# Attention probabilities fetched in three half-key buffers over two loop steps, and the value products ahead of a 512-column query product

## The chip, the cores and the metric

The kernel runs on one core of a Trainium2 chip. The metric is the device time of one execution in microseconds (us); lower is better. TensorE (PE) multiplies matrices, VectorE (DVE), ScalarE (ACT) and GpSimd (POOL) work on elements, and SyncE (SP) issues nearly all DMA transfers of the part that is changed. Each engine takes its instructions in the order of the program.

## The reference

Two layers over x of shape 16 x 256 x 256 (16 sequences of 256 tokens), all in float32. Each is x + s * silu(f), with s and f computed from the layer norm of x. In layer 0, s is a complex linear recurrence and f a two-matrix network with gelu. In layer 1, f is a linear layer with gated low-rank experts, and s is the attention that the change touches:

```
q = x @ Wq                                  # 16 heads of 128 + 64 (rotary)
c_kv, k_rope = x @ Wkv_a                    # 64 latent + 64 rotary columns, shared by the heads
kv = rmsnorm(c_kv) @ Wkv_b                  # keys and values of each head
scores = q . k / sqrt(192), causal mask
attn = softmax(scores)
out = (attn . v) @ Wo
```

The kernel folds Wkv_b into Wq and Wo, so that all heads share one 128-wide key (64 latent, 64 rotary) and one 64-wide value, the latent itself.

## The kernel before

Layer 0 takes the first 270 us or so. Layer 1 is one software pipeline, unrolled by the loop `for i in range(LAST)` (line 1643). A **chunk** is two sequences (512 tokens); there are 8. A **group** is four heads of a chunk; there are 4 per chunk, 32 in all. A **unit** is one group for one of the two sequences, b = 0 or 1. Step i of the loop handles unit i, so even steps have b = 0 and odd steps b = 1, and r = i mod 8 is the place in the chunk. Group m is units 2m and 2m+1.

What a step writes, in program order, as far as it matters here:

1. On odd steps `fetch` of group (i-3)/2, four DMAs on SP.
2. `score_pack(u, 0)`: the **first scores**, two products of 256 and 224 columns into a PSUM bank `sc`; DVE masks them and takes the row maxima, ACT takes exponentials into `pr`.
3. `turn(w, 1)`, `turn(w, 2)`: DVE transposes, by 32 x 32 blocks, two thirds of the normalised probabilities of the unit before, w, into `turned`.
4. `query_mm(n, 3)` on even steps: a **query product** of 512 columns, `pq<-xnT,wlat`; `query_lat` (ACT) moves it to `qg`. (On odd steps it is `query_mm(n, 0)`.)
5. `score_pack(u, 1)`: the **second scores**, 192 + 160 + 128 columns.
6. `turn(w, 0)`, the last third, which follows the second scores in DVE's order, and `send(w)`: four SP DMAs, `far<-turned`, to a DRAM buffer.
7. On even steps `query_move(n)`: eight SP DMAs, `qg<-qrot`, that bring the rotary rows of the queries to their partitions, and then `values_of` of group (i-4)/2.
8. `score_pack(u, 2)`: the **third scores**, 96 + 64 + 32 columns, and then what the place r asks for (`pm`, `pg`, `tp`, `pkv`, `po`).

`far` lays the transposed probabilities out so that a second set of DMAs, `pT<-far`, brings them back with keys on partitions: rows 0 to 63 of `pT` belong to b = 0 and rows 64 to 127 to b = 1. The index y = 0 or 1 tells which 64 keys of each block of 128. `pT` of a group is one tile with one buffer, filled by four DMAs of 384 KB in the order (y, b) = (0,0), (0,1), (1,0), (1,1). `values_of` multiplies it with the values `rowv` in 64 x 64 quarters of the array, for key blocks z = 0 to 3 of 64 keys; block z reads half y = z mod 2. Here z = 0, 1, 2, 3 have 512, 384, 256 and 128 columns:

```
for z, c0 in enumerate((0, 64, S, S + 64)):
    n0 = 64 * z
    heads = q.pT[:, z % 2, :, c0 : c0 + S - n0].rearrange("p (a hh) q -> p a hh q", hh=2)
```

So a group's b = 1 half is sent on step 2m+2, fetched at the start of step 2m+3, and used on step 2m+4. PE's order is fixed by the `InOrder` helper (line 53), and so is that of the other engines; the profile books everything recorded through it under line 53. PSUM has five banks `m1` taken in turn (`pq`, `av`, `po` and others) and three banks `sc`.

Of the kernel before, what the change touches and what calls it, by code (L numbers as in the profile page):

```python
# [11 lines left out]
F32 = mybir.dt.float32  # L12
# [6 lines left out]
P = 128  # L19
B, S, D = 16, 256, 256  # L20
# [21 lines left out]
def tile_two_layers(ctx: ExitStack, tc: tile.TileContext, d: dict, out: bass.AP):  # L42
# [175 lines left out]
    sp = InOrder(nc.sync)  # L218
# [5 lines left out]
    def m1(name, shape):  # L224
        return place["pool"].tile(shape, F32, tag=place["tag"], name=name)
# [84 lines left out]
    def key_chunk(ch):  # L310
        k = chunks[ch]
        pk = m1(f"pk_{ch}", [P, CH])
        for j in range(TPC):
            pe.transpose(pk[:, j * P : (j + 1) * P], k.row[:, j, :], ident)
        k.kT = ak.tile([P, CH], F32, tag="kT", name=f"kT_{ch}")
        ac.copy(k.kT, pk)
# [62 lines left out]
    G = 4  # L379
# [60 lines left out]
    with ExitStack() as l0:  # L440
# [106 lines left out]
        def tiny(name, n=1):  # L547
            return w0.tile([P, n], F32, tag=name, name=name)
# [44 lines left out]
        f = tiny("f")  # L593
# [12 lines left out]
        for k in range(1, 8):  # L606
            c, s = rot[:, k - 1, 0:1], rot[:, k - 1, 1:2]
# [10 lines left out]
        for k in range(8):  # L618
            n = 1 << k
            c, s = rot[:, k, 0:1], rot[:, k, 1:2]  # L620
# [124 lines left out]
        def recur_out(ch, g, w, ve, ge):  # L745

            swapped(w, g)
            h = a2.tile([P, S], F32, tag="hs", name=f"hs_{ch}")
            ve.tensor_tensor(h, g, ct, ALU.mult)
            ge.tensor_tensor(h, h, w, ALU.subtract)  # L750
            return h
# [512 lines left out]
        h = recur_out(ch, g, w, v0, g0)  # L1264
# [35 lines left out]
    pp = ctx.enter_context(tc.tile_pool(name="p1", bufs=2))  # L1300
# [29 lines left out]
    def gate_end(ch, jp):  # L1330
        k = chunks[ch]
        g = k.g2[:, 2 * jp : 2 * jp + 2, :]
        ve.scalar_tensor_tensor(g, g, 1.0, k.h, ALU.add, ALU.mult)
# [31 lines left out]
    def score_pack(u, pi):  # L1365
        k, b, pack = chunks[u.ch], u.b, PACK[pi]
        if pi == 0:
            u.nm = sm1.tile([P, NQ], F32, tag="nm", name=f"nm_{u.n}", bufs=3)
            u.sr = sm1.tile([P, NQ], F32, tag="sr", name=f"sr_{u.n}", bufs=3)
        qg = groups[u.i // 2].qg  # L1370
        sc = ps_sc.tile([P, CH], F32, tag="sc", name=f"sc_{u.n}_{pi}")
        for a, o in pack:
            pe.matmul(
                sc[:, o : o + 32 * (a + 1)], qg[:, b * NQ + a, :, :].rearrange("p h q -> p (h q)"),
                k.kT[:, b * S : b * S + 32 * (a + 1)], start=True, stop=True,
            )
        ends = [o + 32 * (a + 1) for a, o in pack]
        step = ends[1] - ends[0]
        n = len(pack)
        assert ends == [ends[0] + step * z for z in range(n)]  # L1380
        if ends[0] - 32 + step * n <= CH:
            diag = sc[:, ends[0] - 32 : ends[0] - 32 + step * n].rearrange("p (n s) -> p n s", n=n)[:, :, 0:32]
        else:
            diag = sc[:, ends[0] - step : ends[-1]].rearrange("p (n s) -> p n s", n=n)[:, :, step - 32 : step]
        ve.tensor_tensor(diag, diag, bc(kmask, n), ALU.add)
        for a, o in pack:
            ve.tensor_reduce(
                u.nm[:, a : a + 1], sc[:, o : o + 32 * (a + 1)], AX.X, ALU.max, negate=True
            )
        for a, o in pack:  # L1390
            w = 32 * (a + 1)
            ac.activation(
                u.pr[:, OFF[a] : OFF[a] + w], sc[:, o : o + w], AF.Exp,
                bias=u.nm[:, a : a + 1], accum_out=u.sr[:, a : a + 1],
            )

    def normalise(u, packs):
        blocks = [a for pi in packs for a, _ in PACK[pi]]
        lo, hi = min(blocks), max(blocks) + 1
        ve.reciprocal(u.sr[:, lo:hi], u.sr[:, lo:hi])  # L1400
        for a in blocks:
            v = u.pr[:, OFF[a] : OFF[a] + 32 * (a + 1)]
            gp.tensor_scalar(v, v, u.sr[:, a : a + 1], 1.0, ALU.mult, ALU.mult)
# [29 lines left out]
    def new_pT(u):  # L1433
        u.pT = pp.tile([P, G, 3, P], F32, tag="turned", name=f"pT_{u.n}", bufs=2)

    def fetch(n):

        q = groups[n]
        q.pT = pp.tile([P, 2, G, 3 * P], F32, tag="pT", name=f"pT_{n}", bufs=1)
        far = q.far.rearrange("b (y k) s h z q -> y b (k s) (h z q)", y=2)  # L1440
        for y in range(2):
            for b in range(2):
                sp.dma_start(
                    q.pT[64 * b : 64 * b + 64, y].rearrange("p h q -> p (h q)"), far[y, b]
                )

    def turn_here(u, z):

# [32 lines left out]
    def values_of(n):  # L1481

        q = groups[n]
        ch, g = divmod(n, NG)
        k = chunks[ch]
        av = [m1(f"av_{ch}_{g}_{b}", [P, 2, S]) for b in range(2)]
        for z, c0 in enumerate((0, 64, S, S + 64)):
            n0 = 64 * z
            heads = q.pT[:, z % 2, :, c0 : c0 + S - n0].rearrange("p (a hh) q -> p a hh q", hh=2)
            for b in range(2):  # L1490
                rows = slice(64 * b, 64 * b + 64)
                for hh in range(2):
                    pe.matmul(
                        av[b][64 * hh : 64 * hh + 64, :, n0:S], k.rowv[rows, z, :],
                        heads[rows, :, hh, :], start=(z == 0), stop=(z == 3),
                    )
        k.attT.append(a2.tile([P, 2, CH], F32, tag="attT", name=f"attT_{ch}_{g}", bufs=6))
        for b in range(2):
            ac.copy(k.attT[g][:, :, b * S : (b + 1) * S], av[b])
# [143 lines left out]
    for i in range(LAST):  # L1643
        ch, r = divmod(i, PER)
        odd = i % 2 == 1
        u, w = units[i], units[i - 1] if i else None
        here = w is not None and w.i >= LAST - 2
        n = (i + 3) // 2 if odd else (i + 2) // 2
        n = n if n < len(groups) else None
        more = ch + 1 < NCH  # L1650
        last = ch - 1 if ch == NCH - 1 and r in FINISH else None
        fast = ch - 1 if 0 < ch < NCH - 1 else None

        if odd and i > 2:
            fetch((i - 3) // 2)
        score_pack(u, 0)
        if w:
            normalise(w, (2,))
        if fast is not None and r > 3:
            fast_begin(fast, r)  # L1660
        if ch > 1 and r == 0:
            fast_begin(ch - 2, 0)
        out_weights(i)
        if r == 1:
            gate_end(ch, 0)
        if r == 2:
            gate_end(ch, 1)
            if more and ch:
                norm_end(ch + 1)
        if r == 5 and more:  # L1670
            kv_end(ch + 1)
        if i == LAST - 1:

            finish_mm(last, 3, 0, NPAIR)
            finish_out(last, 3)
            last = None
        if w:
            for z in (1, 2):
                turn_here(w, z) if here else turn(w, z)

        if r == 0:
            mid_chunk(ch)
        if r == 7 and more:
            key_chunk(ch + 1)
        if n is not None:
            query_mm(n, 0 if odd else 3)
            if not odd:
                query_lat(n, 3)
        if i == 5:
            values_of(0)  # L1690
        score_pack(u, 1)

        if odd and n is not None:
            query_mm(n, 1)
            query_mul(n, 0)
        if i == 2:
            query_move(n)
        if w:
            if here:
                turn_here(w, 0)  # L1700
            else:
                turn(w, 0)
                send(w)
        if not odd:
            if n is not None and i != 2:
                query_move(n)
            if i > 4:
                values_of((i - 4) // 2)
        score_pack(u, 2)
        normalise(u, (0, 1))  # L1710

        if odd and n is not None:
            query_mm(n, 2)
            query_mul(n, 1)
            query_rot(n)
            query_lat(n, 2)
        if r < 2:
            gate_begin(ch, r)
        if r == 0 and more and ch:
            norm_begin(ch + 1)  # L1720
        if r == 2 and more:
            transpose_chunk(ch + 1)
        if r == 4 and more:
            kv_begin(ch + 1)
        if r == 6 and more:
            router_chunk(ch + 1)
        if last is not None:
            j = FINISH.index(r)
            finish_mm(last, j, 0, NPAIR)
            finish_out(last, j)  # L1730
        if fast is not None and r in FINISH:
            fast_end(fast, r)
# [94 lines left out]
```

## Time and profile before

| | us |
|---|---|
| median of 3 runs (lowest, highest) | 949.57 (947.73, 950.8) |
| the profiled execution, its own time | 946.94 |
| its span, first to last instruction | 945.2 |
| PE busy in the span | 921.8 (98%) |
| DVE, ACT, POOL busy | 665.3, 477.9, 571.6 |
| mean granted TensorE clock | 0.986 of full |

A PE instruction's end is modelled, so "busy" includes time in which PE only waits for the next operand; the distance from one start to the next is the better measure of what a piece of work costs. A float32 product is two passes in the trace, so six `sc` rows are three products. The DMA issues of SP are rows of SPq; a transfer lands some microseconds after its issue. Seven or eight tenths of the DMA engines' time are in use through layer 1.

### The profile page before, as it was taken

What the parts mean: (1) busy time and instruction counts of PE and PEld (TensorE: products, weight loads), DVE (VectorE), ACT (ScalarE), POOL (GpSimd) and SP (SyncE); (2) the same over time, 40 slices, a digit from 0 to 9 for tenths busy, and PEclk for the clock granted to TensorE, in tenths of its full rate; (3) what the DMA queues carried; (4) which work ended last, traced back from release to release, by engine and by line L of the source; (5) the groups of instructions that cost most, each with busy time, mean ns of one, the idle gap of its engine ahead of it and who ended that gap; (6) DMA issues with size and microseconds to landing.
All of it is one profiled execution on the core that took longest, in us unless ns stands there. A gap on an engine that the chain in (4) does not pass through costs nothing.

```text
span 945.2 us, 17425 instructions
## 1 busy us (share of the span) xinstructions
PE 921.8 (98%) x5426; PEld 684.8 (72%) x5426; DVE 665.3 (70%) x2017; ACT 477.9 (51%) x1562; POOL 571.6 (60%) x885
## 2 busy tenths in 40 slices
PE   8999999999999899999999999999999999999988
PEld 7777989996767575776686677667667776766766
DVE  6876678763778688678657857875885787586642
ACT  3334565562446555546536544554555555465431
POOL 1238678775455454877557567657757765775531
PEclk9999999999999899999989999999999999999979
DMA  9630000000027968868767886888778688878880
GB/s 283 214 112 1 1 1 1 1 2 1 1 46 157 231 147 178 193 160 208 195 152 170 192 187 146 196 186 218 166 182 194 157 192 196 210 167 203 187 213 23
DMA packets 197404, 134.00 MB, mean 142 GB/s; under 512 B 143104, under 2 KB 187968, under 8 KB 197312
## 3 DMA queue, kind: packets, MB, share of 16 engines
q1 hardware_dynamic: 195184, 128.69, 57.5%
q0 software_dynamic: 1152, 3.67, 1.1%
q8 instruction: 44, 0.72, 0.3%
q10 hardware_dynamic: 976, 0.53, 0.2%
q14 instruction: 48, 0.39, 0.1%
HBM read 63.11 MB, written 52.95 MB: 123 GB/s over the span
## 4 chain that ended last, share of the span: by engine, by line
PE 68%; DMA 13%; SPq 7%; DVE 6%; POOL 5%; issue 1%; ACT 1%; DVEq 0%; POOLq 0%; ACTq 0%
PE pq L53 13%; DMA pT<-far 12%; PE sc L53 9%; PE po L53 8%; SPq L53 7%; PE r L53 7%; PE f L53 7%; PE av L53 6%; PE ph L53 5%; PE pf L53 4%; PE pg L53 3%; POOL pr L53 2%; PE pkv L53 2%; PE pm L53 1%; PE tp L53 1%
## 5 line engine op out<-in xcount | busy, mean ns | idle before, releaser
L53 POOL TENSOR_SCALAR pr<-pr,sr 128x256 f32<-128x256 f32 (+7 forms) x512 | 192.6, 396 | 213.9 <-DVE sr L53 212.7
L53 ACT ACTIVATE pr<-sc,nm 128x256 f32<-128x256 f32 (+7 forms) x512 | 189.7, 380 | 229.0 <-DVE sr L53 149.1
L53 PEld LDWEIGHTS sc<-kT,qg 128*128 128x128 f32 x1024 | 159.6, 193 | 57.2 <-issue 42.7
L53 PE MATMUL sc<-kT,qg 128*128 128x256 f32 (+7 forms) x1024 | 178.2, 309 | 1.3 <-ACT pr L53 1.3
L53 DVE TENSOR_REDUCE nm<-sc 128x1 f32<-128x256 f32 (+7 forms) x512 | 127.5, 301 | 6.6
L53 DVE STREAM_TRANSPOSE turned<-pr 128x512 f32<-128x512 f32 x186 | 123.2, 687 | 10.5 <-POOL pr L53 10.5
L53 PE MATMUL pq<-xnT,wlat 128*128 128x512 f32 x256 | 122.6, 602 | 0.0
L53 PE MATMUL pq<-xnT,wrope 128*128 128x512 f32 x256 | 120.2, 593 | 0.0
L53 PE MATMUL av<-pT,rowv 64*64 64x512 f32 (+2 forms) x992 | 98.7, 451 | 14.1 <-DMA pT<-far 13.9
L53 DVE TENSOR_TENSOR sc<-sc,kmask 128x96 f32<-128x96 f32 (+1 forms) x192 | 45.9, 239 | 90.6 <-PE sc L53 89.4
L53 ACT ACTIVATION_READ_ACCUMULATOR pr<-sc,nm 128x1 f32 x512 | 103.0, 201 | 0.0
L53 PEld LDWEIGHTS av<-pT,rowv 64*64 64x64 f32 x992 | 44.8, 135 | 64.6 <-DMA pT<-far 36.6
L53 POOL TENSOR_TENSOR qrot<-qmul,qmul 128x512 f32<-128x512 f32 x64 | 83.5, 1326 | 4.2 <-DVE qmul L53 2.8
L53 DVE TENSOR_TENSOR qmul<-pq,rot_q 128x512 f32<-128x512 f32 x128 | 80.8, 672 | 0.1
L53 ACT ACTIVATE qg<-pq 64x512 f32<-64x512 f32 x128 | 75.5, 590 | 4.3 <-PE pq L53 3.5
L53 PEld LDWEIGHTS pq<-xnT,wrope 128*128 128x128 f32 x256 | 45.7, 191 | 32.4 <-issue 32.1
L53 PEld LDWEIGHTS pq<-xnT,wlat 128*128 128x128 f32 x256 | 45.7, 191 | 31.6 <-issue 31.6
L53 PEld LDWEIGHTS po<-wout,attT 128*128 128x128 f32 x416 | 60.7, 198 | 10.0 <-issue 5.0
L53 PE MATMUL po<-wout,attT 128*128 128x128 f32 (+1 forms) x416 | 66.8, 316 | 0.0
L53 POOL TENSOR_TENSOR rs<-ve,mhalf 128x4 f32<-128x4 f32 (+1 forms) x17 | 16.8, 988 | 52.4 <-DVE ve L53 38.5
L53 POOL TENSOR_TENSOR attT<-attT,attT 128x512 f32<-128x512 f32 x36 | 45.1, 1271 | 0.0
L53 PE MATMUL ph<-xnT,p1T 128*128 128x256 f32 (+1 forms) x128 | 44.2, 502 | 0.8 <-DVE xnT L53 0.8
(229 smaller groups left out, 1524.7 us busy)
## 6 DMA issues: line engine op xcount, KB each, us to landing
far<-turned SPq DMA_DIRECT2D x248, 192.0 KB, 4.0
pT<-far SPq DMA_DIRECT2D x124, 384.0 KB, 5.9
qg<-qrot SPq DMA_DIRECT2D x256, 64.0 KB, 2.3
x<-in_x_dram SPq DMA_DIRECT2D x7, 512.0 KB, 9.3
out_dram<-x POOLq DMA_DIRECT2D x12, 256.0 KB, 5.6
wqn_wo<-in_wq_nopeT_dram SPq DMA_DIRECT2D x4, 512.0 KB, 5.1
wqn_wo<-in_Wo_dram SPq DMA_DIRECT2D x4, 512.0 KB, 5.9
p2T<-in_proj2T_dram SPq DMA_DIRECT2D x2, 512.0 KB, 7.7
```

The lines of the kernel that those rows point to most:

```text
L53: r = getattr(self.engine, name)(*args, **kw)
```

## The change

The three parts, and the diff. (1) `pT` becomes two tiles per group, one for each y, from a ring of three buffers. (2) `fetch` now issues one DMA; the four are spread over two steps: (0,0) at the start of even step 2m+2, (1,0) later on that step, behind `values_of` of group m-1, and (0,1) and (1,1) at the start of step 2m+3. (3) `values_of` moves from behind the second scores to a place ahead of `query_mm(n, 3)`, and takes its key blocks in the order 0, 2, 1, 3. The columns of each block, the number of DMAs, their sizes, and the orders of DVE and POOL stay as they are. On ACT the two copies of `av` now stand ahead of the two `query_lat` of the step.

```diff
-    def fetch(n):
+    def fetch(n, y, b):
         q = groups[n]
-        q.pT = pp.tile([P, 2, G, 3 * P], F32, tag="pT", name=f"pT_{n}", bufs=1)
-        far = q.far.rearrange("b (y k) s h z q -> y b (k s) (h z q)", y=2)
-        for y in range(2):
-            for b in range(2):
-                sp.dma_start(
-                    q.pT[64 * b : 64 * b + 64, y].rearrange("p h q -> p (h q)"), far[y, b]
-                )
+        if y == b == 0:
+            q.pT = {}
+        if b == 0:
+            q.pT[y] = pp.tile([P, G, 3 * P], F32, tag="pT", name=f"pT_{n}_{y}", bufs=3)
+        sp.dma_start(
+            q.pT[y][64 * b : 64 * b + 64].rearrange("p h q -> p (h q)"),
+            q.far[b].rearrange("(y k) s h z q -> y (k s) (h z q)", y=2)[y],
+        )
...
-        for z, c0 in enumerate((0, 64, S, S + 64)):
+        for z in (0, 2, 1, 3):
             n0 = 64 * z
-            heads = q.pT[:, z % 2, :, c0 : c0 + S - n0].rearrange("p (a hh) q -> p a hh q", hh=2)
+            c0 = (0, 64, S, S + 64)[z]
+            heads = q.pT[z % 2][:, :, c0 : c0 + S - n0].rearrange("p (a hh) q -> p a hh q", hh=2)
...
         if odd and i > 2:
-            fetch((i - 3) // 2)
+            fetch((i - 3) // 2, 0, 1)
+            fetch((i - 3) // 2, 1, 1)
+        elif i and not odd:
+            fetch((i - 2) // 2, 0, 0)
         score_pack(u, 0)
...
             key_chunk(ch + 1)
+        if i and not odd:
+            if i > 4:
+                values_of((i - 4) // 2)
+            fetch((i - 2) // 2, 1, 0)
         if n is not None:
             query_mm(n, 0 if odd else 3)
...
             if n is not None and i != 2:
                 query_move(n)
-            if i > 4:
-                values_of((i - 4) // 2)
         score_pack(u, 2)
```

## The prediction

> **What bounds the kernel now.** I read the page first: busy times, then the chain that ended last.
>
> ```profile
> PE 921.8 (98%) x5426; PEld 684.8 (72%) x5426; DVE 665.3 (70%) x2017; ACT 477.9 (51%) x1562; POOL 571.6 (60%) x885
> ...
> PE 68%; DMA 13%; SPq 7%; DVE 6%; POOL 5%; issue 1%; ACT 1%; DVEq 0%; POOLq 0%; ACTq 0%
> PE pq L53 13%; DMA pT<-far 12%; PE sc L53 9%; PE po L53 8%; SPq L53 7%; PE r L53 7%; PE f L53 7%; PE av L53 6%; PE ph L53 5%; PE pf L53 4%; PE pg L53 3%; POOL pr L53 2%; PE pkv L53 2%; PE pm L53 1%; PE tp L53 1%
> ```
>
> PE looks full, but an eighth of the chain runs over the landing of `pT`. The waits say who stands there:
>
> ```profile
> PEld av L53 <- DMA pT<-far: 36.6, 38, 2.2
> ...
> PE av L53 <- DMA pT<-far: 13.9, 25, 1.3
> ```
>
> These overlap each other and modelled ends, so I price the waits from starts on the timeline of PE. Two groups, 13 and 14, in one chunk:
>
> ```profile
> 576.68 0.98 PE L53 MATMUL sc<-kT,qg 128*128 128x256 f32 x4
> 577.49 1.88 PE L53 MATMUL pq<-xnT,wlat 128*128 128x512 f32 x4
> 579.21 0.98 PE L53 MATMUL sc<-kT,qg 128*128 128x192 f32 x6
> 580.12 2.38 PE L53 MATMUL av<-pT,rowv 64*64 64x512 f32 x32
> 582.43 0.85 PE L53 MATMUL sc<-kT,qg 128*128 128x96 f32 x6
> ...
> 598.61 1.85 PE L53 MATMUL av<-pT,rowv 64*64 64x512 f32 x12
> 601.21 1.51 PE L53 MATMUL av<-pT,rowv 64*64 64x384 f32 x20 [0.74 <-DMA pT<-far]
> 602.65 0.85 PE L53 MATMUL sc<-kT,qg 128*128 128x96 f32 x6
> ```
>
> Unhindered, a group's value products take 582.43 - 580.12 = 2.31 us; those of group 14 take 602.65 - 598.61 = 4.04, so 1.73 is waiting. Over all 31 groups the time above 2.31 sums to 38.6 us. By the step on which they run, the six full chunks (groups 5 to 28) have on average 0.92 (r=0), 1.51 (r=2), 1.70 (r=4) and 0.00 (r=6): 4.13 per chunk.
>
> Why the data are late, for group 14, on DVE and SP's queue:
>
> ```profile
> 580.23 0.27 DVE L53 TENSOR_TENSOR sc<-sc,kmask 128x96 f32<-128x96 f32 x1 [0.27 <-PE sc L53]
> 580.53 0.79 DVE L53 TENSOR_REDUCE nm<-sc 128x1 f32<-128x192 f32 x3
> 581.23 0.70 DVE L53 STREAM_TRANSPOSE turned<-pr 128x512 f32<-128x512 f32 x1
> ```
>
> ```profile
> 581.96 3.53 SPq L53 DMA_DIRECT2D far<-turned  x4
> 585.65 5.72 SPq L53 DMA_DIRECT2D qg<-qrot  x8
> 591.47 2.49 SPq L53 DMA_DIRECT2D pT<-far  x4
> ```
>
> DVE waits 0.27 us for the second scores, masks and reduces them, and only then turns the last third of the b=1 probabilities (ends 581.93). SP sends them, issues eight `qg` transfers, then fetches. The four fetches land at 596.08, 597.85, 599.56 and 601.16: 4.6 us after issue, then one every 1.7. The last, (1,1), is what PE waited for.
>
> **The change, part by part.**
>
> *Fetch spread.* Of four fetches behind `qg`, the two of b=1 remain. The last needed lands second instead of fourth: two landings, 3.4 us, earlier. The b=0 pair lies earlier in SP's queue. (0,0) waits there for the b=0 `far` writes. In the trace these land up to 7.8 us after what will be the start of the previous products, where four fetches were in flight before them; with two, some 3 us sooner. (1,0) waits for that group's key blocks 0 and 2, done 1.3 us after they start. Queued behind both are the b=1 `far` writes and `qg`, but DVE releases these writes only 6.75 us plus the wait, 8.8 in all, after the products start (below). That turn is the cover, and I cost the new waits at nothing; had the b=0 writes not moved, 7.8 plus two issues of 0.6 would hold `far` back by 0.2, and nothing excludes a gain where DMA engines are freed behind `qg`. The third buffer gives (0,0) a tile that products two groups back have left: no wait.
>
> *Products ahead of the query product.* First scores to products instead of to `pq`: 0.91 against 0.81 (now the second scores pay that 0.10: 579.21 to 580.12); no change. Third scores cost 0.69 behind products and 0.59 behind other scores or `pq` (medians of starts, before the next product); now they follow the second scores: 0.10 saved per group. Products start earlier in their step by 580.12 - 577.59 = 2.53 us; their data must be there that much sooner.
>
> *The second scores are moved too.* They come behind products and `pq`: 2.31 + 1.72 = 4.03 us after the products start, plus whatever the products wait. DVE's order is unchanged, so the last third of the turn still stands behind them. From the second scores' start to its end is 581.93 - 579.21 = 2.72. It therefore ends 6.75 us + wait after the products start. On r=4 and r=6 it ended 1.81 after the old start, so it is 2.41 us later against the other work, plus the wait. On r=0 POOL, and on r=2 DVE's own backlog, set it (3.67 and 4.54 after the old start, 6.20 and 7.07 after the new); a wait of 0.3 or more makes the second scores last there as well.
>
> So there is now a circle: products wait, second scores late, turn late, `far`, `qg`, `pT`, next products. In group 14's numbers: products of 13 at 577.59, `pq` at 579.90, second scores at 581.62, turned at 584.34. Turn to first fetch is 9.54 (591.47 - 581.93) and landing 4.61: data at 598.49 and 1.77 later at 600.26. The products of 14 could start at 595.98 (their old first scores at 594.74, less 0.10, plus 0.81 + 0.43 for `pmT` + 0.10). Wait 2.51. Key blocks 0 and 2 then take 0.87 + 0.39 = 1.26, so the odd half adds 0.51: 3.02 against 1.73 before. Four landings became two, but 2.53 of start and 2.41 of turn went against it.
>
> For all groups: wait = 6.75 + Z - (old start-to-start without wait - 0.10), plus 0.50 for the odd half. Z is turn end to first landing, means of six chunks: 13.22 into r=0, 13.59 into r=2, 13.04 into r=4, 13.1 into r=6. Start-to-start without wait: 18.49, 19.15, 18.37, 22.91. Waits: 1.58 + 0.50, 1.29 + 0.50, 1.52 + 0.50, none. That is 5.89 per chunk, less 0.41 of boundaries: 5.48 against 4.13, **+1.35 per chunk, +8.1 for six**. Outside them: groups 1 to 4 waited 8.07 and by the same sum 7.5, less 0.4 of boundaries; group 28, without its neighbours' fillers, +0.7; group 29, whose steps have no query products any more, 5.78 before and 4.6 after (its start-to-start grows from 14.6 to 15.7 as products move). Together about -1.5. Sum: +6.5 on the profiled 946.94 (945.2 span + 1.7 outside), so 953.4; on the median 949.57, **956.0**.
>
> *Other queues.* ACT copies `av` before `query_lat`: its results are needed a group later, at 51% busy. The second bank of `av` is asked for 2.3 us sooner; on r=0 DVE frees it at 597.2, about 1.1 after the new start: under the wait of 1.6, and up to 1.1 per chunk if that wait vanished. `qg` lands about 10.3 after the turn, 17.0 + wait, against first scores due at 17.5: close, but `pT` comes later anyway.
>
> A rule to weigh is "Overlap DMA with compute" of DMA: Bandwidth & Descriptors (the Trainium skill), in its rules for kernel authors: issue early, wait late. The b=0 half obeys; the b=1 half is waited for earlier and issued later. Taken for all four transfers the rule would clear the 38.6, giving about 908; the rows above give +6.5.
>
> **Rivals.**
>
> *A, the wait goes (faster).* If the late half hid, 38.6 - 5 at the tail and 3 of boundaries would go: about 913. It needs Z below 18.39 - 6.75 - 0.5 = 11.1 into r=0; the shortest there is 12.5. Against it: DVE's 0.27 wait on the second scores.
>
> *B, the circle is shorter (same or slightly faster).* Hiccups in SP's issue make 8.2 into 9.6 us, and less DMA traffic stands behind the late half. With the shortest Z of each kind (12.47, 13.29, 12.72) waits are 0.83 + 0.99 + 1.20 + 1.50 = 4.52, less 0.41: 4.11, equal to 4.13; 948 with the ends. With the shortest issue (8.2) and landing (4.2) together, 12.4 everywhere: 0.76 + 0.10 + 0.88 + 1.50 less 0.41, 2.83 per chunk, -7.8 for six and -1.5 outside: 940.
>
> *C, the clock (slower).* Waits near 2.5 to 3 can halve PE's clock. Group 8 waited 2.78, and then:
>
> ```profile
> 470.00:480.00 10.00, 9.28 (x59) 8.05 (x56) 2.23 (x11) 2.86 (x12) 4.49 (x8) 0.66 0.86 219
> ```
>
> The clock was 0.66 and the next products came 3.0 us later than in other chunks. Three groups would wait over 2.5 now (6, 8, 14): +3 to +9, up to 965.
>
> *D, the change does not do what it says:* excluded, since the orders of PE and SP are written out by hand and both do change.
>
> **How the numbers follow.** About 0.3% (2.8 us) is what a measurement tells from no change. The circle has 0.47 and C on top of it 0.15; both are slower, 952.5 to 966, which is the forecast's own range. B's middle (0.13) is within 0.3%; B's short end (0.15) and A (0.10) are faster. 940 to 966 takes in B and leaves out A and some worse clock, about 0.17.
>
> **What would show it.** After the change: first scores, products, `pq`, second scores in this order on PE; products still waiting for `pT<-far` on r=0, 2 and 4, about 2 us each, none on r=6; start-to-start near 20.5 us for these three; the last third of the turn 2.7 us behind the second scores and 6.75 + wait behind the products; SP's `far` to `pT` still 8.2 to 9.6; third scores 0.59. Wrong if waits on r=0 fall below 0.5, if the turn does not move with the second scores, or if SP's stretch shrinks below 8.

## The result and the profile after

The changed kernel takes 963.25 us (median of 4 runs, 961.62 to 965.49); the kernel before, measured beside it, 948.65 (945.16 to 950.8). The ratio is 1.016, with a 95% interval of 1.012 to 1.020: 14.6 us slower. The profiled execution took 961.62, with a span of 959.8.

The page of the changed kernel, busy times and the chain that ended last:

```profile
PE 928.1 (97%) x5426; PEld 676.8 (71%) x5426; DVE 664.7 (69%) x2017; ACT 480.4 (50%) x1562; POOL 570.7 (59%) x885
...
PE 62%; DVE 10%; DMA 10%; SPq 8%; POOL 4%; ACT 2%; issue 2%; ACTq 0%; DVEq 0%
```

The work is the same, but less of the chain lies on PE (62% after 68%), and DVE has risen from 6% to 10%, most of all by the row maxima behind the second scores (`DVE nm`, 2% of the chain). PE's timeline of groups 13 and 14:

```profile
587.46 2.38 PE L53 MATMUL av<-pT,rowv 64*64 64x512 f32 x32
589.77 1.98 PE L53 MATMUL pq<-xnT,wlat 128*128 128x512 f32 x4
591.59 1.57 PE L53 MATMUL sc<-kT,qg 128*128 128x192 f32 x12
...
605.95 1.08 PE L53 MATMUL av<-pT,rowv 64*64 64x512 f32 x4
607.33 2.71 PE L53 MATMUL av<-pT,rowv 64*64 64x512 f32 x28 [0.30 <-DVE qmul L53]
609.97 1.98 PE L53 MATMUL pq<-xnT,wlat 128*128 128x512 f32 x4
```

The products of group 13 did not wait (2.31 us), those of group 14 took 609.97 - 605.95 = 4.02, a wait of 1.71. Between the two starts lie 18.49 us. DVE after group 13's products:

```profile
592.61 0.27 DVE L53 TENSOR_TENSOR sc<-sc,kmask 128x96 f32<-128x96 f32 x1 [2.78 <-PE sc L53]
...
593.61 0.70 DVE L53 STREAM_TRANSPOSE turned<-pr 128x512 f32<-128x512 f32 x1
```

and SP's queue:

```profile
594.34 2.18 SPq L53 DMA_DIRECT2D far<-turned  x4
596.62 5.86 SPq L53 DMA_DIRECT2D qg<-qrot  x8
602.52 1.27 SPq L53 DMA_DIRECT2D pT<-far  x2
```

DVE stands 2.78 us idle for the second scores, where it stood 0.27 before, and the turn ends 6.85 us after the products' start (594.31 - 587.46). Turn to `pT` is 8.2 us, the short end of the 8.2 to 9.6 of the kernel before.

On r=0, where group 14 runs, the products have a second wait. Their fifth row starts at 607.33, 0.10 us behind the end of `qmul` on DVE (607.23), while the first of the late halves had landed at 607.11:

```profile
605.98 1.25 DVE L53 TENSOR_TENSOR qmul<-pq,rot_q 128x512 f32<-128x512 f32 x2
```

The fifth row is the first that writes the second PSUM bank of `av`, whose release by DVE the prediction has under *Other queues*. Groups 10, 14, 22 and 26 all go on 0.10 us behind `qmul`. In qg_first (below) the first late half of groups 10, 22 and 26 lands 0.7 us or more before that moment and the second before its rows come up, and the products still wait 1.37 or 1.38 us. So of the mean wait of 1.61 us on r=0 in the changed kernel, 1.37 would stay if the data came early: about 8 us over the six full chunks that the late data are not needed to explain.

I add up two waits of PE over layer 1. *Product waits* are the time of the value products above 2.31 us, as in the prediction. *`qg` waits* are the time by which the first scores of an even step start later than PE's own work allows, counted where they start 0.30 to 0.45 us behind the landing of their last `qg` transfer. A group's `qg` wait is that of the step on which its products run.

| us | products before | products after | `qg` before | `qg` after |
|---|---|---|---|---|
| groups 1 to 4 | 8.1 | 8.7 | 1.4 | 9.1 |
| groups 5 to 28 | 24.8 | 32.7 | 0.0 | 2.0 |
| group 29 | 5.8 | 4.4 | 0.0 | 2.2 |

Together that is 40.1 before and 59.1 after, +19.0. Of the 14.6 that the spans differ by, 1.2 arose in layer 0, which is the same in both. The other -5.6 are time at a lower clock. By the granted clock in their traces both kernels have some 24 us at half clock in layer 1, but in the kernel before more of that fell on work which the table doesn't count: 2.0 us behind group 1 (this kernel lost 1.0 just ahead of it), 3.0 behind group 8 and 1.9 behind group 29, 5.9 in all by the starts on PE.

### The profile page after: what moved, and what is told of

Its sections match the earlier page's. It is cut to its first block, busy times and chain, and to the rows that moved or that the text cites. A ratio compares the mean times of both kernels' runs of the same rounds, so it can differ in the third digit from the quotient of the medians.

```text
span 959.8 us, 17417 instructions
## 1 busy us (share of the span) xinstructions
PE 928.1 (97%) x5426; PEld 676.8 (71%) x5426; DVE 664.7 (69%) x2017; ACT 480.4 (50%) x1562; POOL 570.7 (59%) x885
## 4 chain that ended last, share of the span: by engine, by line
PE 62%; DVE 10%; DMA 10%; SPq 8%; POOL 4%; ACT 2%; issue 2%; ACTq 0%; DVEq 0%
PE pq L53 11%; DMA pT<-far 10%; SPq L53 8%; PE av L53 7%; PE sc L53 7%; PE r L53 7%; PE f L53 7%; PE po L53 6%; PE ph L53 5%; PE pf L53 4%; POOL pr L53 3%; PE pg L53 3%; DVE nm L53 2%; ACT pr L53 2%; PE pkv L53 1%
## 5 line engine op out<-in xcount | busy, mean ns | idle before, releaser
L53 PEld LDWEIGHTS sc<-kT,qg 128*128 128x128 f32 x1024 | 157.1, 193 | 64.1 <-issue 51.4
L53 PE MATMUL sc<-kT,qg 128*128 128x256 f32 (+7 forms) x1024 | 171.3, 306 | 11.9 <-DMA qg<-qrot 8.4
L53 PE MATMUL pq<-xnT,wlat 128*128 128x512 f32 x256 | 125.6, 613 | 0.0
L53 PE MATMUL av<-pT,rowv 64*64 64x512 f32 (+2 forms) x992 | 107.7, 465 | 12.0 <-DMA pT<-far 9.4
L53 PEld LDWEIGHTS po<-wout,attT 128*128 128x128 f32 x416 | 58.4, 191 | 9.4 <-issue 3.5
L53 PE MATMUL po<-wout,attT 128*128 128x128 f32 (+1 forms) x416 | 64.2, 308 | 0.0
L53 ACT COPY attT<-av 128x512 f32<-128x512 f32 x63 | 33.9, 592 | 40.4 <-PE av L53 40.3
L53 POOL TENSOR_TENSOR rs<-ve,mhalf 128x4 f32<-128x4 f32 (+1 forms) x17 | 16.8, 988 | 52.5 <-DVE ve L53 41.5
```

Source lines behind the costliest of these rows:

```text
L53: r = getattr(self.engine, name)(*args, **kw)
```

## The experiments

Times are medians beside the kernel before in the same measurement; 949 stands for it in sums.

### The second scores ahead of the products (scores_first)

```diff
+        if not odd:
+            score_pack(u, 1)
         if i and not odd:
             ... values_of, fetch (1,0)
...
-        score_pack(u, 1)
+        if odd:
+            score_pack(u, 1)
```

> The changed kernel, but on even steps the second scores stand ahead of the value products (first scores, second scores, products, query product). Fetches, buffers and all else as changed. Theory 1 (a circle: products wait, second scores late, turn late, far, qg, pT): the turn now ends 3.5 us after the first scores whatever the products do; first landing about 15.3 us after the products start against 18.4 and more to the next, so the waits on r=0, 2 and 4 fall below 0.3 us each and the time to 915 to 932. Theory 2 (the DMA engines carry too much, the order on PE does not matter): waits as before, 958 to 966. Theory 3 (only the earlier need counts, not the turn): products stand 0.9 us later in the step than in the changed kernel, so each of 22 waits falls by 0.9, about 943.

931.83 us, ratio 0.981 (0.978 to 0.984). Everything else is the change: spread fetches, ring, products ahead of the query product. PE's timeline:

```profile
587.49 0.98 PE L53 MATMUL sc<-kT,qg 128*128 128x192 f32 x6
588.40 2.79 PE L53 MATMUL av<-pT,rowv 64*64 64x512 f32 x32
591.13 1.98 PE L53 MATMUL pq<-xnT,wlat 128*128 128x512 f32 x4
```

The products start later by the 0.9 us of the second scores, but the turn ends 3.2 us (r=4, 6), 5.4 (r=0) or 5.8 us (r=2) after their start, not 6.9 plus their wait. Product waits fall from 45.9 to 16.2 and `qg` waits from 13.3 to 8.2. The time is at the upper edge of Theory 1; the waits are 0.41 (r=0), 0.63 (r=2) and 0.54 (r=4), above its 0.3. The 0.41 is the same in all six chunks, and PE goes on 0.10 us behind `qmul` there, with the half it needs long landed: it is the bank again, and up to 6 of the 31 us that this kernel gains come from asking for the bank later. For the rest the order cuts the circle at one place. The rate of the DMA engines can't explain the gain: the same bytes move. So the circle is shown on r=2 and r=4; on r=0 it is one of two waits that end almost together.

### The products behind the second scores again (old_place)

```diff
-        if i and not odd:
-            ... values_of, fetch (1,0)
         if n is not None:
             query_mm(n, 0 if odd else 3)
 ...
         score_pack(u, 1)
+        if i and not odd:
+            ... values_of, fetch (1,0)
```

> The changed kernel with its products of values back behind the second scores, together with the (1,0) fetch: on PE first scores, query product, second scores, products, third scores, as in the kernel before; on SP the spread order of the changed kernel, unchanged. Theory 1 (circle): the turn no longer waits for the products. It ends 1.8 (r=4, 6), 3.7 (r=0) or 4.5 us (r=2) after the products' start instead of 6.9 plus the wait; with 13.2 from turn to landing all waits of the six full chunks go (24.8 us), some 4 of groups 1 to 4 and 2 of group 29; the start stays 4 us late. 915 to 928, waits below 10 us in sum. Theory 2: it is the products in front that make spread fetches useful, or the head waits of (0,0) and (1,0) hold the b=1 writes here as they did on step 4: waits of 1 us or more on r=2 and r=4, 932 to 945. Theory 3 (the DMA engines' rate sets when data land): 948 or more.

922.36 us, ratio 0.974 (0.970 to 0.977). PE's timeline, and the chain:

```profile
587.06 1.88 PE L53 MATMUL pq<-xnT,wlat 128*128 128x512 f32 x4
588.78 0.98 PE L53 MATMUL sc<-kT,qg 128*128 128x192 f32 x6
589.69 2.38 PE L53 MATMUL av<-pT,rowv 64*64 64x512 f32 x32
592.00 0.85 PE L53 MATMUL sc<-kT,qg 128*128 128x96 f32 x6
```

```profile
PE 87%; DVE 4%; DMA 3%; POOL 3%; SPq 2%; issue 1%; ACT 1%; POOLq 0%; DVEq 0%; ACTq 0%
```

Product waits are 6.2 us in all, and the chain lies on PE for 87%. Theory 1 holds, with the sum it gave. So the change is two things of opposite sign: ring, key order and spread fetches are worth -27 us, and on top of them the place of the products +41.

### The place of the products alone (products_only)

```diff
 (in the kernel before)
+        if i > 4 and not odd:
+            values_of((i - 4) // 2)
         if n is not None:
             query_mm(n, 0 if odd else 3)
...
-            if i > 4:
-                values_of((i - 4) // 2)
```

> The kernel before, with the value products alone moved ahead of the query product; fetch, its four DMAs, its one buffer and the order of key blocks as before. Theory 1: the same circle with the fourth landing in it: waits of 5.7, 5.4, 5.6 and 1.2 us on r=0, 2, 4 and 6, 18 per chunk against 4.1, so 1050 or more, 1110 with halved clocks. Theory 3 (only the earlier need counts): 2.5 us more on three of four groups, about 1005. Theory 2: 949 to 960.

1111.79 us in one run, at a mean clock of 0.907. Without the spread fetches the circle carries all four landings: the waits of the six full chunks are on average 5.5, 5.5, 5.5 and 1.4 us on r=0, 2, 4 and 6, where the sum had 5.7, 5.4, 5.6 and 1.2. Product waits are 135 us, 97 more than before; the other 66 us or so go with the lower clock and were not parted further.

### The ring and the key order alone (ring_only), and two buffers in place of three (two_buffers)

ring_only is the kernel before with the new `fetch` and `values_of`, called as before:

```diff
-            fetch((i - 3) // 2)
+            if i != 5:
+                for y in range(2):
+                    for b in range(2):
+                        fetch((i - 3) // 2, y, b)
...
             values_of(0)
+            ... the same four fetches of group 1
```

> The kernel before with one part of the change: pT as two tiles a group from a ring of three, and key blocks in the order 0, 2, 1, 3. All four fetches stay together at the start of the odd step and the products behind the second scores (group 1's fetches behind the products of group 0, where their buffer comes free). Theory 1: without the spread the fourth landing stays where it was, 4.6 + 5.1 us behind the first issue, so the waits of r=0, 2 and 4 stay; only what is left to do after the last landing shrinks, from key blocks 1, 2, 3 (1.44 us) to 1 and 3 (1.05), 0.4 us for each of some 22 waiting groups: 938 to 944. Theory 2 (the third buffer, not the spread, is what old_place gained by): 918 to 930.

938.41, ratio 0.987 (0.982 to 0.992): the time lies in the range of Theory 1, at its lower edge. Product waits are 33.3 against 38.6, 5.3 us less where Theory 1 counted some 9, and 12% of the chain still is the landing of `pT`. The step from here to old_place, 16 us by the medians and 13 by the ratios, is the spread.

two_buffers is old_place with `bufs=2`, both b=0 fetches behind the products, and the start of old_place_back (below):

```diff
...
             values_of((i - 4) // 2)
+            fetch((i - 2) // 2, 0, 0)
             fetch((i - 2) // 2, 1, 0)
...
```

> old_place_back (920.26) with two buffers in place of three, that is, with no more room than the kernel before. (0,0) of a group then needs a tile that the products of the same step empty, so both b=0 fetches stand behind the products in SP's queue: (0,0) can go 1.3 us and (1,0) 2.3 us after the products start, and the b=1 far writes at 2.9 or later, where old_place_back had them at 2.1 to 4.5. Theory 1 (the gain is the order of SP's queue, and the products hardly wait): 919 to 926. Theory 2 (the third buffer carries the gain, since far and qg are held by up to 1 us on every even step and the first scores wait for qg): 930 or more.

923.5, ratio 0.972 (0.966 to 0.977), and 0.971 for old_place_back: in this order the third buffer is worth nothing that these runs can tell. `qg` waits rise to 14.7 from the 11.3 of old_place_back, which is the price of the held queue in the trace.

### The first groups (ring_start, start_back, old_place_back, scores_back)

In the changed kernel SP's queue on steps 4 and 5, and what PE does there:

```profile
305.89 2.54 SPq L53 DMA_DIRECT2D far<-turned  x4
312.54 1.10 SPq L53 DMA_DIRECT2D pT<-far  x2
313.69 3.31 SPq L53 DMA_DIRECT2D far<-turned  x4
317.10 5.39 SPq L53 DMA_DIRECT2D qg<-qrot  x8
```

```profile
324.61 1.94 PE L53 MATMUL sc<-kT,qg 128*128 128x256 f32 x4 [6.33 <-DMA qg<-qrot]
326.48 5.21 PE L53 MATMUL av<-pT,rowv 64*64 64x512 f32 x32
```

The b=1 third was turned at 309.3, but (0,0) stood ahead of it in the queue, waiting for the b=0 writes to land. `far` and `qg` went 4.4 us late, the first scores of step 6 waited 6.3 us, and the products after them ran at a granted clock of 0.68 (325 to 335 us): they took 5.1 us and ended 2.8 us behind their last landing, where the odd half takes 1.05. By step, the changed kernel is 1.2 us behind the kernel before at step 5, 6.3 at step 6 and 8.3 at step 13, of 14.7 at the end. My first theory was that the (1,0) fetch of group 1 waits for a buffer of the ring:

```diff
-        fetch((i - 2) // 2, 1, 0)
+        if i != 4:
+            fetch((i - 2) // 2, 1, 0)
 ...
             values_of(0)
+            fetch(1, 1, 0)
+            fetch(1, 1, 1)
```

> The changed kernel, but on step 4 the fetch of group 1's half (1,0) is left out, and both halves (1,0) and (1,1) of that group are fetched on step 5 behind the first value products. Theory 1 (the head of the queue): at step 4 that one DMA waits for a buffer that the first value products free only on step 5, and holds the far and qg transfers behind it; so the 6.3 us wait for qg before the first scores of step 6 falls below 1.5 us, and the time falls by 3 to 6 us from 963, to 957 to 960. Rival (the late start is paid by the halved clock and the DMA engines, not by that wait): step 6 stays 4 us or more late, 961 to 966.

961.26, ratio 1.012 (1.010 to 1.015), with step 6 at 323.43, 1.2 us earlier. A miss, and what the rival gave: in the changed kernel (1,0) went at 313.1, directly behind (0,0) at 312.54, so it held the queue for little more than its own issue; (0,0) had held it before. So start_back moves both b=0 fetches of the first two groups behind `far` and `qg`, and two other kernels got the same edit (here the new places alone; group 1's y=1 fetches go as in ring_start):

```diff
         if not odd:
             query_move(n)
+            if i == 2 or i == 4:
+                fetch((i - 2) // 2, 0, 0)
+            if i == 2:
+                fetch((i - 2) // 2, 1, 0)
```

> The changed kernel; only its first two groups get the b=0 half of the probabilities later: on steps 2 and 4 the fetches (0,0) and (1,0) do not stand ahead of the b=1 far writes and the qg transfers in SP's queue, but behind both (group 1's two y=1 fetches on step 5, behind the products of group 0). Theory 1, after ring_start: in the changed kernel (0,0) of group 1 waits at the head of the queue for the b=0 far writes to land (312.47) while the b=1 probabilities were turned at 309.3, so far and qg run 4.4 us late and the first scores of step 6 start at 324.6 instead of 319.5; ring_start took only the wait for the buffer away, not this one. Then here step 6 starts as in the kernel before (318 to 320), and 3 to 6 us of the changed kernel's loss go: 957 to 960 against 963.25, or 8.5 to 11.5 above the kernel before. Theory 2: the late start of step 6 has another cause (less DMA issued early, or qrot late), or the steady circle takes it back: 961 to 965, with step 6 still at 323 or later.

961.35, ratio 1.017 (1.013 to 1.020). The start of step 6 came as Theory 1 said and the gain did not: step 6 starts at 319.81, on time, but group 1's products then wait 4.84 us instead of 2.83, and steps 8 and 12 wait 2.03 and 2.22 for `qg` instead of 1.61 and 0.98. Both waits of groups 1 to 4 sum to 15.3 instead of 17.8. About 2.0 of these 2.5 us were given back at a lower clock:

```profile
320.00:325.00 5.00, 3.37 (x14) 1.11 (x15) 3.12 (x8) 2.84 (x12) 5.00 (x10) 0.67 1.01 234
325.00:335.00 10.00, 10.00 (x52) 5.32 (x45) 1.34 (x5) 2.45 (x5) 0.23 (x1) 0.65 0.70 189
```

The granted clock (third number from the end) was 0.65 to 0.67, and the first scores of step 6 took 2.7 us to the products (1.9 in the changed kernel), `pq` behind them 3.0 (1.8). At step 13 the kernel is 8.6 us behind, against 8.3.

> old_place with the first two groups' b=0 fetches behind far and qg, as in start_back. Theory 1: 3 to 6 us below old_place, 911 to 924, the best of all; step 6 starts at 318 to 320. Theory 2: as old_place within 1.5 us.

> scores_first (second scores ahead of the products, 931.83) with the first two groups' b=0 fetches behind far and qg, as in start_back. Theory 1: 3 to 6 us below scores_first, 926 to 929. Theory 2: 930 to 933. Beside old_place_back it tells what the query product's place behind the products is worth when the second scores are ahead of both: by the circle old_place_back is faster by the waits that scores_first kept on r=0, 2 and 4 (about 1.4 us per chunk, 8 to 10 in all), since its products start 1.7 us later in their step.

920.26 (0.971, 0.968 to 0.974) against old_place's 922.36, and 931.88 against 931.83: no gain that these runs can tell. But the two kernels differ by 11.6 us. In both the second scores are ahead of the products; this is what it is worth to have the query product ahead of them instead of behind the products. old_place_back, old_place and two_buffers are the fastest kernels here, and these runs do not tell them apart.

### qg ahead of far (qg_first), and qg from another queue (qg_act, old_place_qg)

The circle runs through the eight `qg` issues. qg_first puts them in front of the `far` writes:

```diff
                 turn(w, 0)
+                if not odd and n is not None and i != 2:
+                    query_move(n)
                 send(w)
         if not odd:
-            if n is not None and i != 2:
+            if n is not None and i == 0:
                 query_move(n)
```

> The changed kernel, but the eight qg transfers of an even step are issued ahead of the four far transfers instead of behind them. Theory 1: SP is idle for some 6 us while the turn is under way, so these issues go there; from turn to first landing falls from 13.1 to about 7.5 us, the waits on r=0, 2 and 4 go, 915 to 932. Theory 2 (DMA engines full): bytes and engines are the same, so 955 to 966.

980.24, ratio 1.033 (1.030 to 1.036): the opposite of what I expected. SP's queue and the turn it serves (DVE):

```profile
575.14 1.09 SPq L53 DMA_DIRECT2D pT<-far  x2
576.33 7.97 SPq L53 DMA_DIRECT2D qg<-qrot  x8
584.40 2.48 SPq L53 DMA_DIRECT2D far<-turned  x4
589.64 1.14 SPq L53 DMA_DIRECT2D pT<-far  x2
```

```profile
578.18 0.70 DVE L53 STREAM_TRANSPOSE turned<-pr 128x512 f32<-128x512 f32 x1
```

`far` to `pT` shrank as hoped, on average from 8.5 to 5.3 us from first to first. But `qg` itself can't start before (0,0) and (1,0) have left the queue, and lasts 8 us, so `far` went 2.7 to 5.1 us after its turn (means by place), where it had gone at once. Late `far` makes the next b=0 writes and (0,0) late, and so the next `qg`. I had counted the queue behind the turn and forgotten that the queue in front of it is in the circle as well.

qg_act issues them from ACT (`ac.dma_start` for `sp.dma_start` in `query_move`), old_place_qg does the same to old_place.

> The changed kernel with the eight qg transfers of a group issued by ACT instead of SP, at the same place of the program. In SP's queue the b=1 far writes are then followed at once by (0,1) and (1,1). Theory 1 (the circle, closed by two things that stand behind the turn, pT and qg): turn to first landing falls from 13.2 us to about 10.5 (2.2 to issue the far writes, 3 to 3.6 until they land, 4.6 for pT). The waits 6.86 + 10.5 - 18.4 + 0.5 are below zero, so the product waits of the six full chunks (33 us in the changed kernel) and the first scores' waits for qg (about 11) go, and the time is 918 to 932, as much better as ACT allows. Theory 2: ACT is the price. Eight issues of 0.5 to 0.65 us each are some 5 us per group during which the exponentials of the third scores stand still; POOL's normalising and the turn are then late by as much, and the product waits stay at 1 us or more: 940 to 975. Theory 3 (the DMA engines' rate, not the queue, sets when data land): turn to first landing stays above 12.5 and the time within 955 to 968.

> old_place (922.36) with the eight qg transfers issued by ACT. In old_place the product waits are gone (6.2 us in sum) and what PE still waits for is mostly qg, at the first scores of even steps: they start 0.30 us after its last landing on steps 6, 8, 12, 20, 28, 36 and 60 to 62. Theory 1: with qg out of SP's queue these go: 908 to 918. Theory 2 (ACT's 5 us per group are the price): 922 to 950.

1049.06 (1.105, 1.097 to 1.113) and 987.66 (1.039, 1.033 to 1.045). Only the direction of Theory 2 was right; both lie beyond its range. ACT and SP in qg_act:

```profile
632.86 5.29 ACTq L53 DMA_DIRECT2D qg<-qrot  x6
638.20 0.34 ACT L53 ACTIVATE pr<-sc,nm 128x96 f32<-128x96 f32 x1 [5.71 <-DMA qg<-qrot]
```

```profile
631.81 6.41 SPq L53 DMA_DIRECT2D far<-turned  x4
```

ACT's exponentials stand still for 5.7 us here, while it issues, and the four `far` issues on SP beside that take 6.5 us (median) where they took 2.2 in the changed kernel. The `far` issues of the same run that have no `qg` issue beside them take 2.2 as well. Turn to first `pT` issue is 9.7 to 10.4 us instead of 8.4 to 8.7, so the stretch that was to shrink grew. The Trainium skill, Perfetto Trace Analysis, in "DMA Optimizations", says that it may help to balance DMAs across the engines that can issue them when descriptor generation is the bottleneck; here the second issuer slowed the first. These two runs thus say nothing on the circle.

## Why the prediction was right and wrong

**The circle: right in kind, and near in its total.** PE's order, the turn behind the second scores (6.86 us plus the wait after the products' start; 6.75 was forecast), 8.1 to 9.5 us from turn to `pT`, waits on r=0, 2 and 4 and none on r=6 are all in the trace. Start-to-start is 18.7, 20.8 and 19.9 us into these three, not near 20.5 for each: into r=0 it holds no wait, since r=6 has none. Groups 5 to 28 wait 32.7 + 2.0 = 34.7 us; the sum had 6 x 5.89 + 0.7 = 36.0. By place, product waits are 1.61, 1.46 and 2.39 where it had 2.08, 1.79 and 2.02, so the total agrees better than its parts, and on r=0 the bank alone would make 1.37 of the 1.61: that much of the agreement is luck. The `qg` waits belong in it: `qg` and `pT` hang on the same turn, so where PE stops first only says at which place the same wait is spent. scores_first and old_place show the cause by taking it away, and products_only by making it larger, with the waits that the sum gives.

**The size of the whole: wrong**, 14.6 us measured where 6.5 were forecast. That 963.25 lies below 966 is luck too: the upper part of the range was for rival C, a lower clock behind groups 6, 8 and 14, and the time went elsewhere. The steps that failed:

- *"Groups 1 to 4 waited 8.07 and by the same sum 7.5"*: they waited 17.8 (9.5 before, with `qg`), 8.9 us of the miss. Of the 17.8, 9.1 were waits for `qg`, which *"close, but `pT` comes later anyway"* had put at nothing. For groups 2 to 4 the same sum holds if it is made with their own rows: 6.86 + Z + 0.5 less start-to-start without waits is 3.4, 2.1 and 3.4, and 3.3, 2.0 and 3.2 were measured. From group 1 to group 2 start-to-start is 16.8 us, not 18.5, because the first chunk has no `po` (1.8 us) of an earlier one to do there; before, that mattered to nothing. Group 1 is the rest, 9.3, and there another step failed:
- *"That turn is the cover, and I cost the new waits at nothing"*: it holds in the steady chunks, where the b=1 writes leave 0.03 us behind the turn. On step 4 no products stand ahead of the second scores (group 0's run on step 5), the turn was early, and the queue held it for 4.4 us. start_back shows that hold, and that undoing it alone gains no time that can be told.
- *"0.10 saved per group"*, 2.9 us, did not come. `pq` behind the products takes 1.82 us where it took 1.72: the third scores' 0.10 only changed its place.
- Group 29, *"5.78 before and 4.6 after"*: 4.4 + 2.2 = 6.6, 2.0 us of the miss. Its products ended 3.4 us behind their last landing, at a granted clock of 0.50 (920 to 925 us); that is rival C, in a place that I had not given it, though the kernel before shows 0.50 there too (910 to 915 us).

These are 13.8 us, and 1.2 of layer 0. Against them stand the 5.6 us of clock and the 1.3 us that groups 5 to 28 waited less than the sum, which leaves the 8.1 of the miss.

**The rivals.** A needed Z below 11.1 and B the shortest Z, 12.5 to 13.3; the means are 13.1 to 13.3. The rule weighed, "Overlap DMA with compute" of DMA: Bandwidth & Descriptors (the Trainium skill), describes half of the change: the spread without the moved products gave 922 us, the whole 963. Moving the products does not let the late half be issued earlier: its source waits for the products of the group before.

## What to carry to other kernels

When a step is moved ahead, list what it pushes back and follow that to the data of the step's own next turn: if it closes a circle, the wait is the sum around it less the work of one turn, and starting earlier only makes it longer. Make that sum with the rows of every place, the first and the last turns above all, where the work that fills a turn is missing and a queue has no cover. And part the change: here one part was worth -27 us and the other +41.

## What was not expected of the hardware

- Two engines issuing DMAs at a time did not add up: in qg_act the 28 sets of four `far` issues on SP that ran beside ACT's `qg` issues took 6.0 to 7.4 us, and the 32 sets that did not took 2.2 (median).
- A change of PE from 64 x 64 to 128 x 128 products cost 0.10 us in the block behind it: third scores 0.69 instead of 0.59, `pq` 1.82 instead of 1.72.
- First scores that wait for `qg` start 0.30 us behind its last landing on six of the steps of the changed kernel, to the hundredth. Such waits can be told in the trace even where its releaser names another engine.
- The clock fell behind some waits of 2 us and not behind others: 0.50 behind group 29's (2.0 for `qg`, then 0.7 for `pT`), 0.68 (562 to 566 us) behind group 12's, 1.55 us in one piece, and 1.00 (600 to 640) behind group 14's 1.7, which is a sum of short pieces. What the clock goes by is not shown here.
